# Weaving the transform, the encoder and the last layer of one group into the absolute differences of the next

## The chip, the cores and the metric

One Trainium2 chip, one core. The time is the device time of one execution in microseconds (us). The engines are named as in the profile: PE is TensorE, PEld its weight loads, DVE VectorE, ACT ScalarE, POOL GpSimd; SP is the engine that issues most DMA transfers (524 of 610 in the trace of the kernel before), and its queue (SPq) is called the Sync queue here. The profile's "granted clock" is TensorE's clock as a share of full speed.

## The reference, cut to what matters

An input of 16 batches, 32 channels, 128 x 128, in fp32, goes through four layers, each added to its input after a group normalisation.

```python
x = x + L0(gn(x))    # a row-by-row LSTM
x = x + L1(gn(x))    # absolute differences: out[n,f,i,j] = -sum over c,kh,kw of |q(x) patch - q(w)|
x = x + L2(gn(x))    # 2-D Hartley transform, mixing of 32 x 32 modes, transform back
x = x + L3(gn(x))    # 25 shifted products per channel, 3x3 convolutions with pooling down and up, times x
```

L1 has no product that TensorE could do. For each output channel and tap, VectorE or ScalarE makes relu(q(x) - w) over 128 partitions x 8192 elements (sums of relu and linear terms give the absolute difference), and TensorE only adds the channels up. That is 72 differences for each of 32 halves (16 batches, upper and lower half), 2304 in all. L2 normalises over two channels of one batch and L3 over the same, so what follows L1 can start as soon as a batch is done; the kernel works it off in four groups of four batches.

## The kernel before: the parts that matter

The stages run one after another. In the stage of the differences a batch is first quantised (ScalarE scales, VectorE rounds and clips, the result goes to DRAM with a border), then each half loads its quantised rows four times over, once for each quarter of the partitions.

```python
def jc_rows(t, b, half, n=16 * W):      # 4 blocks of 16 rows x 32 channels -> 128 partitions
    return bass.AP(t.tensor, t.offset + b * CHW + half * 64 * W, [[16 * W, 4], [HW, C], [1, n]])
...
def loaded(b, half):
    q = qp.tile([128, R + 2, P], F16, name="q")
    first = q_d.offset + (b * C * (H + 2) + R * half) * P
    nc.sync.dma_start(q, bass.AP(q_d.tensor, first, [[0, 4], [(H + 2) * P, C], [1, (R + 2) * P]]))
    xr = rp.tile([128, 16 * W], F32, name="xr1")            # the residual, two halves buffered
    nc.sync.dma_start(xr, jc_rows(x1, b, half))
    return q, xr
...
for b in range(B):
    for half in range(2):
        q, xr = following
        following = loaded(b + half, 1 - half)              # (but for the last half)
        if half == 0 and b + 1 < B:
            xq = [unquantised(b + 1, i) for i in range(2)]  # 16 rows each
        ...                                                 # linear terms
        for i in range(72):
            act = i % 4 == 3
            if i == 3 and before:
                finish(*before)                             # residual + sums, statistics, store
            ...                                             # the difference, on ACT or DVE; 16 matmuls
            if i in (10, 30) and half == 0 and b + 1 < B:
                quantise(b + 1, int(i == 30), xq[int(i == 30)])
        before = b, half, acc, xr
```

Of the kernel before, what the change touches and what calls it, by code (L numbers as in the profile page):

```python
# [209 lines left out]
def jc_stats(nc, pool, ps, cst, v, name):  # L210

    rhs = pool.tile([128, NG, 4], F32, name=f"{name}_r")
    nc.vector.tensor_tensor(rhs, bcast(v[:, :], 2, 4), bcast(cst["m4_bc"], 1, NG), ALU.mult)
    p = ps.tile([128, 512], F32, name="acc")
    nc.tensor.matmul(p[:, :16], cst["sel_c"], rhs.rearrange("p g b -> p (g b)"), start=True, stop=True)
    out = pool.tile([128, 16], F32, name=name)
    nc.vector.tensor_copy(out, p[:, :16])
    return out


def jc_rows(t, b, half, n=16 * W):

    return bass.AP(t.tensor, t.offset + b * CHW + half * 64 * W, [[16 * W, 4], [HW, C], [1, n]])


def stage1(nc, tc, keep, cst, sel16, m1, r1, x1, w, q_d, x2):
# [8 lines left out]
    with ExitStack() as ctx:  # L235
        sm = ctx.enter_context(tc.tile_pool(name="s1_sm", bufs=1))
        with tc.tile_pool(name="s1_ps0", bufs=2, space=PSUM) as ps:
            r128 = jc_stats(nc, sm, ps, cst, r1, "r128")
            shift = jc_stats(nc, sm, ps, cst, m1, "shift")
            nc.vector.tensor_scalar(r128, r128, 128.0, None, ALU.mult)  # L240
            nc.vector.scalar_tensor_tensor(shift, shift, -1.0, r128, ALU.mult, ALU.mult)


            qw = sm.tile([128, 72], F32, name="qw")
            nc.sync.dma_start(qw, w)
            top = sm.tile([128, 1], F32, name="top")
            nc.vector.tensor_reduce(top, qw, AX.X, ALU.max, apply_absolute_value=True)
            alltop = sm.tile([128, 1], F32, name="alltop")
            nc.gpsimd.partition_all_reduce(alltop, top, 128, bass_isa.ReduceOp.max)
            scale = sm.tile([128, 1], F32, name="scale")  # L250
            nc.vector.tensor_scalar(scale, alltop, 1.0 / 127.0, 1e-8, ALU.mult, ALU.max)
            nc.vector.tensor_scalar(scale, scale, 2.0**0.5, None, ALU.mult)
            nc.vector.tensor_scalar(scale.bitcast(I32), scale.bitcast(I32), 0x7F800000, None, ALU.bitwise_and)
            nc.vector.reciprocal(scale, scale)
            nc.vector.tensor_scalar(qw, qw, scale, -127.0, ALU.mult, ALU.max)
            nc.vector.tensor_scalar(qw, qw, 127.0, RND, ALU.min, ALU.add)
            nc.vector.tensor_scalar(qw, qw, RND, None, ALU.subtract)
            neg = sm.tile([128, 72], F32, name="neg")
            nc.vector.tensor_scalar(neg, qw, -1.0, None, ALU.mult)


            taps = sm.tile([128, 8], F32, name="taps")
            nc.vector.tensor_reduce(taps, qw.rearrange("p (f t) -> p f t", t=9), AX.X, ALU.add)
            tapb = sm.tile([128, 8, 4], F32, name="tapb")
            nc.vector.tensor_tensor(tapb, bcast(taps[:, :], 2, 4), bcast(cst["m4_bc"], 1, 8), ALU.mult)
            sumw = sm.tile([128, 1], F32, name="sumw")
            p = ps.tile([128, 512], F32, name="acc")
            for j in range(4):
                nc.tensor.matmul(
                    p[32 * j : 32 * j + 32, :1],  # L270
                    tapb.rearrange("p f b -> p (f b)"),
                    cst["ones"][:, :1],
                    start=True,
                    stop=True,
                )
            nc.vector.tensor_scalar(sumw, p[:, :1], 2.0**-7, None, ALU.mult)

        stat = sm.tile([128, B, 8, 6], F32, name="stat2")
        ring = [sm.tile([128, 16, P], F16, name=f"qt{i}") for i in range(2)]
        for t in ring:  # L280
            nc.gpsimd.memset(t, 0.0)
        for row in (0, H + 1):
            nc.sync.dma_start(
                bass.AP(q_d.tensor, q_d.offset + row * P, [[4 * (H + 2) * P, 128], [(H + 2) * P, 4], [1, P]]),
                ring[0].rearrange("p r w -> p (r w)")[:, : 4 * P].rearrange("p (a w) -> p a w", w=P),
            )
        xp = ctx.enter_context(tc.tile_pool(name="s1_x", bufs=2))
        rp = ctx.enter_context(tc.tile_pool(name="s1_r", bufs=2))
        qp = ctx.enter_context(tc.tile_pool(name="s1_q", bufs=2))
        dp = ctx.enter_context(tc.tile_pool(name="s1_d", bufs=2))  # L290
        ps = ctx.enter_context(tc.tile_pool(name="s1_ps", bufs=4, space=PSUM))

        def unquantised(b, half):
            t = xp.tile([128, 16 * W], F32, name="xq")
            nc.sync.dma_start(t, jc_rows(x1, b, half))
            return t

        def quantise(b, half, t):
            nc.scalar.activation(
                t, t, AF.Identity, bias=shift[:, b : b + 1], scale=r128[:, b : b + 1]  # L300
            )
            qt = ring[half]
            nc.vector.tensor_scalar(
                qt[:, :, 1 : W + 1], t.rearrange("p (r w) -> p r w", w=W), RND, RND, ALU.add, ALU.subtract
            )
            flat = qt.rearrange("p r w -> p (r w)")
            nc.vector.tensor_scalar(flat, flat, -127.0, 127.0, ALU.max, ALU.min)
            first = q_d.offset + (b * C * (H + 2) + 64 * half + 1) * P
            nc.sync.dma_start(
                bass.AP(q_d.tensor, first, [[16 * P, 4], [(H + 2) * P, C], [1, 16 * P]]), flat  # L310
            )

        def loaded(b, half):
            q = qp.tile([128, R + 2, P], F16, name="q")
            first = q_d.offset + (b * C * (H + 2) + R * half) * P
            nc.sync.dma_start(q, bass.AP(q_d.tensor, first, [[0, 4], [(H + 2) * P, C], [1, (R + 2) * P]]))
            xr = rp.tile([128, 16 * W], F32, name="xr1")
            nc.sync.dma_start(xr, jc_rows(x1, b, half))
            return q, xr

        def finish(b, half, acc, xr):
            v = [xr[:, 512 * k : 512 * k + 512] for k in range(4)]
            for k in range(4):
                nc.vector.scalar_tensor_tensor(v[k], acc[k], sumw, v[k], ALU.subtract, ALU.add)  # L324
            for k in range(4):
                nc.vector.bn_stats(stat[:, b, 4 * half + k, :], v[k])
            nc.sync.dma_start(jc_rows(x2, b, half), xr)

        for half in range(2):
            quantise(0, half, unquantised(0, half))  # L330
        before = None
        following = loaded(0, 0)
        for b in range(B):
            for half in range(2):
# [19 lines left out]
                for i in range(72):  # L354
# [3 lines left out]
                    if i == 3 and before:  # L358
                        finish(*before)
# [191 lines left out]







# [641 lines left out]
```

## Time and profile before

The median is 8975 us (8941 to 8980). In the profiled execution (8962.7 us) L0 lasts until 1510 us, the differences until 5692, the rest until 8963.

### The profile page before, as it was taken

How to read it: one execution, taken by the hardware profiler on the slowest of the kernel's cores; microseconds unless marked ns; L12 is line 12 of the kernel's file. 1: busy time of each engine (PE TensorE's matmuls, PEld its weight loads, DVE VectorE, ACT ScalarE, POOL GpSimd, SP SyncE). 2: the span in 40 equal slices, each digit the busy share in tenths (PEclk: the TensorE clock that was granted, in tenths of full speed). 3: DMA queues.
4: the chain of work that ended last, by engine and by line, in shares of the span. 5: the costliest groups of instructions: out<-in, count | busy, mean ns of one | idle time of the engine just before them, and what ended most of it. 6: DMA issues, size and time to landing. Idle time of an engine off the chain costs nothing.

```text
span 8962.7 us, 249632 instructions
## 1 busy us (share of the span) xinstructions
PE 6114.4 (68%) x117740; PEld 4037.0 (45%) x117740; DVE 5850.7 (65%) x5842; ACT 5003.2 (56%) x2710; POOL 268.8 (3%) x483
## 2 busy tenths in 40 slices
PE   4999991666666656665665666784656859678955
PEld 3888881222222222222222223584644646455832
DVE  5444432999999999999999999622633232232233
ACT  1444432999999999999999999400000101101122
POOL 0111110000000000000000000000000000000000
PEclk9999995999999999999999999755556859688977
DMA  9799923111111111111111110344721121211077
GB/s 205 53 80 78 82 24 80 42 46 42 42 51 54 44 44 52 39 43 48 54 49 43 41 40 25 121 101 115 244 67 43 37 59 43 59 34 34 27 184 170
DMA packets 1520672, 613.85 MB, mean 68 GB/s; under 512 B 1418269, under 2 KB 1421725, under 8 KB 1491613
## 3 DMA queue, kind: packets, MB, share of 16 engines
q1 hardware_dynamic: 1480636, 518.56, 31.2%
q10 hardware_dynamic: 39008, 79.32, 3.0%
q8 instruction: 922, 15.11, 0.7%
q14 instruction: 106, 0.86, 0.0%
HBM read 433.21 MB, written 164.64 MB: 67 GB/s over the span
## 4 chain that ended last, share of the span: by engine, by line
issue 41%; PE 37%; DVE 14%; ACT 3%; DMA 3%; SPq 1%; another core or an unknown queue 0%; POOL 0%; ACTq 0%; DVEq 0%; POOLq 0%
PE acc L952 10%; DVE d_dve L367 7%; PE pg L174 5%; PE pg L175 4%; PE acc L693 4%; PE acc L612 3%; PE pg L176 3%; PE p L426 2%; ACT d_act L365 2%; PE acc L840 2%; PE pf L526 1%; DVE xr L324 1%; DVE stat L200 1%; PE pa L506 1%; PE p L432 1%
## 5 line engine op out<-in xcount | busy, mean ns | idle before, releaser
L365 ACT ACTIVATE d_act<-q,neg 128x8192 f16<-128x8192 f16 (+1 forms) x576 | 4065.9, 7150 | 54.7 <-PE acc L372 29.9
L367 DVE TENSOR_SCALAR d_dve<-q,qw 128x8192 f16<-128x8192 f16 (+1 forms) x1728 | 3935.0, 2365 | 55.6 <-PE acc L372 32.6
L372 PE MATMUL acc<-d_dve,sel 128*32 128x512 f16 x27648 | 1854.7, 391 | 1317.7 <-DVE d_dve L367 1315.9
L372 PEld LDWEIGHTS <-sel 128*32 128x32 f16 x36864 | 1077.8, 98 | 2786.0 <-issue 2082.7
L952 PE MATMUL acc<-xp,fo_all 32*32 32x512 f32 x25600 | 932.4, 624 | 53.1 <-DVE pooled L853 48.5
L952 PEld LDWEIGHTS acc<-xp,fo_all 32*32 32x32 f32 x25600 | 661.4, 105 | 313.7 <-issue 157.5
L372 PE MATMUL acc<-d_act,sel 128*32 128x512 f16 x9216 | 648.0, 401 | 161.5 <-ACT d_act L365 161.1
L185 ACT ACTIVATE gt<-pg,bias 128x256 f32<-128x256 f32 x1024 | 400.9, 474 | 547.5 <-PE pg L176 547.4
L174 PE MATMUL pg<-h,bd 128*128 128x256 f32 x2048 | 652.7, 401 | 57.8 <-DVE h L194 57.5
L175 PE MATMUL pg<-h,bd 128*128 128x256 f32 x2048 | 623.4, 387 | 0.0
L864 ACT ACTIVATE y<-pooled,fo_b 32x128 f32<-32x128 f32 x256 | 102.4, 400 | 842.8 <-DVE pooled L853 839.4
L980 DVE TENSOR_TENSOR acc<-acc,cut 128x4 f32<-128x4 f32 x256 | 28.7, 166 | 696.4 <-PE acc L952 695.4
L693 PE MATMUL acc<-xp 32*32 32x108 f32 x16384 | 326.8, 376 | 222.1 <-issue 217.1
L176 PE MATMUL pg<-xn,bd 128*128 128x2 f32 (+62 forms) x2048 | 426.1, 289 | 9.6 <-DVE xn L158 9.6
L176 PEld LDWEIGHTS pg<-xn,bd 128*128 128x128 f32 x2048 | 397.2, 194 | 66.8 <-DVE xn L158 10.4
L175 PEld LDWEIGHTS pg<-h,bd 128*128 128x128 f32 x2048 | 398.3, 194 | 56.9
L189 DVE TENSOR_TENSOR c<-c,gt 128x256 f32<-128x256 f32 x256 | 108.6, 424 | 448.7 <-ACT gt L185 448.7
L664 DVE TENSOR_SCALAR xp<-xp,stats 128x2560 f32<-128x2560 f32 (+1 forms) x64 | 101.0, 1580 | 446.9 <-DMA xp<-x_d 446.9
L693 PEld LDWEIGHTS acc<-xp 32*32 32x32 f32 x16384 | 250.4, 134 | 298.8 <-issue 271.1
L174 PEld LDWEIGHTS pg<-h,bd 128*128 128x128 f32 x2048 | 341.9, 195 | 64.7 <-issue 48.4
L347 PE MATMUL acc<-q,sel 32*32 32x512 f16 x4608 | 183.8, 594 | 228.6 <-DVE xr L324 135.0
L669 ACT COPY xp<-xp 128x20 f32<-128x20 f32 x64 | 14.9, 233 | 554.6 <-DVE xp L664 442.8
(234 smaller groups left out, 4693.7 us busy)
## 6 DMA issues: line engine op xcount, KB each, us to landing
xr<-x_d SPq DMA_DIRECT2D x96, 1024.0 KB
q<-q_d SPq DMA_DIRECT2D x32, 2145.0 KB
xp<-x_d SPq DMA_DIRECT2D x48, 1280.0 KB
x_in<-in_x_dram SPq DMA_DIRECT2D x16, 2048.0 KB
res<-in_x_dram SPq DMA_DIRECT2D x32, 1024.0 KB
x_d<-res SPq DMA_DIRECT2D x32, 1024.0 KB
xq<-x_d SPq DMA_DIRECT2D x32, 1024.0 KB
x_d<-xr SPq DMA_DIRECT2D x32, 1024.0 KB
```

The source lines that it names most:

```text
L174: nc.tensor.matmul(pg[:, q], wmat(0, q), h_in[:, :, 1:], start=True, stop=False)
L175: nc.tensor.matmul(pg[:, q], wmat(1, q), h_in[:, :, :H], start=False, stop=False)
L176: nc.tensor.matmul(pg[:, q, :, : t + 1], wmat(2, q), xn[:, 2 * c : 2 * c + 2, j, : t + 1], start=False, stop=True,)
L185: nc.scalar.activation(gt[:, q], pg[:, q], AF.Tanh if q == 3 else AF.Sigmoid, bias=bias[:, q : q + 1])
L347: nc.tensor.matmul(acc[k][32 * j : 32 * j + 32, :], sel16[rows, 8, :], q[rows, row : row + 4, kw : kw + W], start=tap == 0, stop=False,)
L365: nc.scalar.activation(dst, src, AF.Relu, bias=neg[:, i : i + 1])
L367: nc.vector.tensor_scalar(dst, src, qw[:, i : i + 1], 0.0, ALU.subtract, ALU.max)
L372: nc.tensor.matmul(acc[k][32 * j : 32 * j + 32, :], sel16[:, f8, :], d[:, row : row + 4, c : c + W], start=False, stop=i == 71,)
L426: nc.tensor.matmul(p1[:, i, :], xh[:, 16 * half + i, :], cst["cas"], start=True, stop=True)
L612: nc.tensor.matmul(acc[blk][32 * j : 32 * j + 32, : rows * n], self.w[part, par, tap, :], src[part, top : top + rows, left : left + n], st ...
L693: nc.tensor.matmul(gram[blk][32 * j : 32 * j + 32, at : at + 36 * n], xp[rows, l, 2 + 32 * j : 34 + 32 * j], xp[rows, l : l + n, 32 * j : ...
L952: nc.tensor.matmul(acc[blk][32 * j : 32 * j + 32, :], wf["all"][rows, tap, :], xp[rows, 4 * j + kh : 4 * j + kh + 4, kw : kw + W], start=t ...
```

## The change

The work after L1 becomes a generator, and a scheduler lets it go on a little after each difference, by a credit of TensorE time; negative values are holds, so that a dependent piece comes only after a number of differences.

```diff
+class Weave:
+    def advance(self, us, slack):
+        self.credit = min(self.credit + slack, 3.0)
+        self.hold = max(self.hold - us, 0.0)
+        if self.credit < 2.0:
+            return
+        while self.credit > 0 and not self.hold and self.step():
+            pass
+DVE_US, ACT_US, PE_US = 2.26, 7.05, 0.87
...
+                    weave.advance(1.75, 1.75 - PE_US)      # after each difference
...
+        first.run(tc, ctx, weave)                          # the differences
+        weave.drain()                                      # what is left
```

The woven work needs room in SBUF, and so the stage of the differences was rewritten too: pieces of 8 rows in the place of 16, residuals for one half in the place of two, loaded inside the half, three VectorE buffers in the place of four, and the choice of engine by an estimate that counts the woven work.

```diff
-            t = xp.tile([128, 16 * W], F32, name="xq")
+        t = self.xp.tile([128, 8 * W], F32, name="xq")
...
-                    following = loaded(b + half, 1 - half)          # q and residual
-                if half == 0 and b + 1 < B:
-                    xq = [unquantised(b + 1, i) for i in range(2)]
+                    following = self.loaded(b + half, 1 - half)     # q alone
...
+                    if i == 30:
+                        xr = self.residual(b, half)
+                    if half == 0 and b + 1 < B:
+                        if i in (4, 6, 26, 28):
+                            k = (4, 6, 26, 28).index(i)
+                            xq[k] = self.unquantised(b + 1, k)
+                        if i in (20, 24, 40, 44):
+                            k = (20, 24, 40, 44).index(i)
+                            self.quantise(b + 1, k, xq[k])
-                    act = i % 4 == 3
-                    d = dp.tile([128, R, P], F16, name="d_act" if act else "d_dve", bufs=2 if act else 4)
+                    act = weave.act + ACT_US < weave.dve + DVE_US and i < 70
+                    t = dp.tile([128, R, P], F16, name="d_act" if act else "d_dve", bufs=2 if act else 3)
```

The rest of the diff (about 1,700 lines) turns the transform, encoder and last layer into generators of one group with four PSUM banks; it is cut here.

## The prediction

> **What bounds the kernel now.** I read the page first (the slices say which engine is full when), then a table of stretches cut where the stages change, then the groups by shape, then the timeline of TensorE in one group. The four rows of the stretches are the stages: absolute differences (1510 to 5692), transform (to 6470), encoder (to 8594), last layer. Columns: stretch, its length, busy us with instructions for PE, PEld, DVE, ACT, POOL, granted clock, DMA share, GB/s.
>
> ```profile
> PE   4999991666666656665665666784656859678955
> DVE  5444432999999999999999999622633232232233
> ACT  1444432999999999999999999400000101101122
> PEclk9999995999999999999999999755556859688977
> 1510.00:5692.00 4182.00, 2567.51 (x41460) 1182.94 (x41464) 4141.00 (x2049) 4122.26 (x605) 0.00 (x0) 0.94 0.15 44
> 5692.00:6470.00 778.00, 540.90 (x10524) 515.36 (x10516) 286.48 (x366) 32.42 (x45) 7.56 (x50) 0.50 0.54 160
> 6470.00:8594.00 2124.00, 1578.71 (x54284) 1145.82 (x54285) 643.67 (x1878) 242.05 (x644) 30.52 (x170) 0.75 0.18 49
> 8594.00:8963.00 369.00, 220.68 (x5334) 108.11 (x5311) 128.16 (x160) 89.00 (x128) 0.00 (x0) 0.76 0.82 191
> ```
>
> For 4182 us VectorE and ScalarE are full and TensorE is 61% busy; for the next 3271 us it is the reverse, VectorE 32% and ScalarE 11% busy. That is the intent: put the second kind of work under the first. The groups that fill the first stretch, and the two of the second that matter most:
>
> ```profile
> L365 ACT ACTIVATE d_act<-q,neg 128x8192 f16<-128x8192 f16 (+1 forms) x576 | 4065.9, 7150 | 54.7 <-PE acc L372 29.9
> L367 DVE TENSOR_SCALAR d_dve<-q,qw 128x8192 f16<-128x8192 f16 (+1 forms) x1728 | 3935.0, 2365 | 55.6 <-PE acc L372 32.6
> L952 PE MATMUL acc<-xp,fo_all 32*32 32x512 f32 x25600 | 932.4, 624 | 53.1 <-DVE pooled L853 48.5
> L693 PE MATMUL acc<-xp 32*32 32x108 f32 x16384 | 326.8, 376 | 222.1 <-issue 217.1
> ```
>
> There are 1728 + 576 = 2304 differences. By busy time over count one costs VectorE 2.277 us and ScalarE 7.058 us; together they do 1/2.277 + 1/7.058 = 0.581 per us, so 2304 need 3967 us. Other work in this stage (evictions, statistics, quantising) is 226 us on VectorE and 66 on ScalarE. Balanced, T = 3967 + 0.756 D + 0.244 A, where D and A are the other work: 3967 + 171 + 16 = 4154, against 4182 measured. I use this formula for the new stage. Last, TensorE in one group's encoder (start, length, matmuls, idle before):
>
> ```profile
> 7046.42 27.72 PE L952 MATMUL acc<-xp,fo_all 32*32 32x512 f32 x782 [1.12 <-DVE pooled L853]
> 7078.39 27.56 PE L952 MATMUL acc<-xp,fo_all 32*32 32x512 f32 x750 [1.04 <-DVE pooled L853]
> ...
> 7193.98 2.54 PE L693 MATMUL acc<-xp 32*32 32x108 f32 x128 [2.01 <-issue]
> 7197.45 2.54 PE L693 MATMUL acc<-xp 32*32 32x108 f32 x128 [0.93 <-issue]
> ```
>
> The first convolution takes 32 us a chunk of which 28 is matmul; the Gram statistics come in bursts of 128 matmuls, 2.5 us of work each 3.5 to 5 us.
>
> [...] each burst ends in a gap put down to issue. From L693, (327 + 222)/16384 is 33 ns per matmul against 20 ns busy. [...] The differences use 128*32, the woven work mostly 32*32; before has no such alternation, so its trace does not price it. [...] The trace shows 0.94 beside the differences and 0.50 in the transform, though the transform keeps TensorE busy 70% of the time; woven, this work should run at the high clock. [...]
>
> **The change part by part.**
>
> 1. How much is woven. A generator emits transform, encoder and last layer of a group between differences, by credit (0.88 us of TensorE work per difference) and holds. I counted the compiled order: in the stream of differences lie preparing the weights once, group 0 whole, and group 1 without its last layer. After the last difference come group 1's last layer and groups 2 and 3 whole, 20802 of 39634 woven matmuls. Group 0 can start only when its four batches are done, a quarter in, and each group takes some 12 of the 32 halves. So at most about half of the 3271 us can be hidden. The split of differences becomes 1700 to 604.
>
> 2. What it adds to VectorE and ScalarE in the first stage. Per group, from counts in the compiled order times durations by shape in the trace before (or scaled by size from them): mean subtraction 4 x 4.42 = 18; inverse transform 32 x (0.685 + 0.682) = 44; Gram sums 40 halves of about 0.6 = 24; folded weights about 15; pooling 40 x 0.69 + 2 = 29; spreading 40; edge corrections 64 x 0.166 = 11; last layer 64 x 0.45 = 29; small pieces 35: 245 us on VectorE. ScalarE: normalising 16 chunks, moved there from VectorE, about 2.6 each by the 2.09 us of a 2048-wide activation = 42; spreading 50; last layer 25 + 18; the rest 12: 147 us. Preparing: 93 us on VectorE once, in place of folding per group. In the stage: D gains 93 + 2 x 245 - 29 = 554 and A gains 2 x 147 - 43 = 251, so T gains 0.756 x 554 + 0.244 x 251 = 480 us: 4182 becomes 4660.
>
> 3. Stalls, my estimate. Five loads of folded weights (1.47 MB each) stand directly ahead of the VectorE instructions that use them: 35 to 40 us a group. Each of 16 chunk loads stands directly ahead of ScalarE's normalisation: some 8 us each, 130 a group. Some 60 evictions a group follow the matmuls they wait for, half of them in the same burst, about 2 to 3 us: 100. By the same weights, 0.756 x 140 + 0.244 x 130 = 137 a group, but part overlaps and buffers absorb part: 190 for both groups. TensorE: 16 sums back to back take 0.87 us, so with 0.88 of woven work per 1.9 us it is above 90% busy, with 487 returns to the differences' tiling; no separate addition. Stage: 4850, from 1510 to 6360.
>
> 4. The tail, groups 2 and 3. Before, a group cost (778 + 2124 + 369)/4 = 818 us, with groups overlapping each other and eight PSUM banks. Now a group is serial with four banks and two buffers. Transform: four batches at 17 us plus load and statistics 92; round trips of coefficients through DRAM 17; mixing 57 (twice the matmuls of before over all groups, 4096 instructions of 14 ns); then 27 for storing and small-run loads, 35 first inverse, 75 second (16.8 MB at 225 GB/s), 10 statistics: 313 against 195. Encoder: first chunk 12, Gram 133, sums 28, constants 8, folded weights 35, chunk 12, edge 13, eight chunks of 33.5 with exposed eviction 268, rest 100 with exposed eviction: 609 against 531. Last layer: 20 store and load, 95 rounds, 10 end: 125 against 92. Sum about 1030 to 1050. Tail: 2 x 1030 + 125 = 2185.
>
> Sum: 1510 + 4850 + 2185 = 8545; I say 8540, 4.8% under 8975.
>
> **The rivals.** (a) Weaving nearly free: the stalls of step 3 are absorbed, and the tail costs a group what it did before: 1510 + 4660 + 2 x 818 + 92 = 7900. For it: TensorE's 39% idle time and the holds put between dependent pieces. Against: the encoder's own waits (842.8 us of ScalarE waiting for pooling) show chains of short steps that a lone group exposes. (b) In-order blocking: each late woven piece stops VectorE, ScalarE and TensorE in turn, and the woven 24 halves take 170 us rather than 152 (131 before): stage 5200 or more, tail 2250, total 8950, no gain. For it: TensorE and VectorE are both above 90%. Against: three VectorE buffers hold 7 us of slack. [...] (d) DMA: at 44 GB/s in the first stage against 191 to 310 elsewhere there is room.
>
> **Range and chances.** Steps 2 and 1 are firm to 100 us. Step 3 may be 0 to 500, step 4 from 1750 to 2350. Taking most of both: 8150 to 8900. Faster by 2% is under 8796; that needs steps 3 and 4 not to overrun by 250 together: 0.80. Within 2%: 0.15. Slower: 0.05.
>
> **What would show it.** The last difference near 6360 (step 3 wrong if under 6200 or over 6600); then no differences and 2100 to 2250 us with VectorE under a third busy. Halves with only differences near 131 us, woven ones near 152. VectorE idle before the folded weights and ScalarE idle before the normalisation, both released by DMA, in the woven stretch. Granted clock above 0.9 until 6360. Gram bursts in the tail again with issue gaps. I am wrong if the woven halves fill VectorE to 99% (then (a)) or if a tail group takes near 818 us.

## More of the kernel before

The lines that show what is full in each stage are in the prediction. One more is kept here, because it was seen and passed over: the waits of the Sync queue in the stage of the differences (engine and line, released by what, us in all, times, longest).

```profile
SPq L318 <- DMA x_d<-xr: 1223.5, 30, 44.3
```

Once a half, the queue stands for about 41 us at the residual load, until the previous half's result has been stored. One such wait as a stretch of its own (columns as in the prediction; the last three are the granted clock, the DMA share and GB/s):

```profile
2201.00:2243.00 42.00, 29.49 (x498) 13.90 (x475) 42.00 (x25) 40.31 (x7) 0.00 (x0) 0.87 0.25 71
```

VectorE is busy for all 42 us and ScalarE for 40, so the wait costs nothing in the kernel before; the DMA engines are 25% busy throughout. The halves there all take 124 to 137 us (from the start of one half's evictions to the next).

## The result, and the profile after

The changed kernel takes 9418.8 us (9410 to 9420): slower, by a ratio of 1.050 (95% interval 1.0475 to 1.0528). A ratio here is the mean time of one kernel's fast runs over that of the other's of the same rounds, so it isn't quite the ratio of the medians.

The slices of the page of the changed kernel, to be held against those in the prediction (40 slices of 235 us; tenths):

```profile
PE   5999973465445654579977765558987646864496
DVE  5444435697776676699978877678997122222212
ACT  2444425697776676699987777678997001210112
PEclk9999987788787787789988787878998557855597
```

Before, DVE and ACT stand at 9 from one end of the differences to the other. Now they reach 9 in some slices only and fall to 6 and 7 between them, PE with them, so nothing is full there. The stretches, cut at the last difference (columns as in the prediction):

```profile
1483.00:7247.00 5764.00, 3801.75 (x78701) 1817.66 (x78707) 4572.60 (x3424) 4579.03 (x1070) 0.00 (x0) 0.83 0.21 63
7247.00:9418.00 2171.00, 1392.84 (x41749) 1030.97 (x41738) 491.05 (x1198) 327.08 (x504) 0.00 (x0) 0.66 0.33 91
```

The tail is what was predicted (2171 us; predicted 2185). The stretch of the differences is 5764 us, not 4850, although DVE and ACT are busy for only 4573 and 4579 us of it, 79%. The two rows of differences (busy, mean ns, idle before and its releaser) say that their own durations are what they were:

```profile
L463 ACT ACTIVATE d_act<-q,neg 128x8192 f16<-128x8192 f16 (+1 forms) x604 | 4278.0, 7151 | 571.4 <-PE acc L404 534.0
L467 DVE TENSOR_SCALAR d_dve<-q,qw 128x8192 f16<-128x8192 f16 (+1 forms) x1700 | 3906.5, 2357 | 491.4 <-PE acc L404 457.3
```

So each of the two waits for some 1190 us of the stretch (5764 - 4573). The waits (engine, what it was about to do, released by what; us in all, times, longest):

```profile
ACT d_act L463 <- PE acc L404: 534.0, 75, 51.2
ACT xq L361 <- DMA xq<-x_d: 489.6, 25, 55.6
DVE d_dve L467 <- PE acc L404: 457.3, 134, 48.4
DVE qt L364 <- DMA q_d<-qt: 323.6, 15, 56.1
```

The second and fourth are no waits of woven work. They are the differences' own quantising: ScalarE waits for the rows to be loaded, VectorE for the previous rounded piece to be stored, each time for up to 56 us. The first and third are also up to 50 us long, and follow from them: TensorE adds the two engines' differences up in one order, so each engine's stop becomes the other's (at 2548, below, TensorE has stood 51 us for VectorE's next difference). The timeline of one half's start shows how (start, length, engine, line, what; in brackets the idle time before and its releaser):

```profile
2481.45 0.50 SPq L376 DMA_DIRECT2D q<-q_d  x1
2487.28 1.84 SPq L394 DMA_DIRECT2D x_d<-xr  x2
2526.84 5.44 SPq L383 DMA_DIRECT2D xr<-x_d  x2
2532.37 0.54 SPq L368 DMA_DIRECT2D q_d<-qt  x1
2533.00 0.53 SPq L356 DMA_DIRECT2D xq<-x_d  x1
...
2544.80 0.70 DVE L364 TENSOR_SCALAR qt<-xq 128x1024 f16<-128x1024 f32 x1 [49.51 <-DMA q_d<-qt]
...
2549.83 1.24 ACT L361 ACTIVATE xq<-xq,shift,r 128x1024 f32<-128x1024 f32 x1 [54.59 <-DMA xq<-x_d]
```

At 2481 the load of the next half's quantised image goes out, at 2487 the stores of the finished half. The residual load needs those stores' buffers, and the queue stands for 38 us at it. The piece store and the piece load stand behind it in the queue; VectorE and ScalarE stand 50 and 55 us at the pieces, and start no difference until these have come (2545.88 and 2550.97), although TensorE had added up the ones before by 2497. The same moment in the kernel before:

```profile
2194.07 0.51 SPq L316 DMA_DIRECT2D q<-q_d  x1
...
2200.67 0.54 SPq L327 DMA_DIRECT2D x_d<-xr  x1
...
2205.21 2.37 DVE L303 TENSOR_SCALAR qt<-xq 128x2048 f16<-128x2048 f32 x2
...
2243.69 0.51 SPq L318 DMA_DIRECT2D xr<-x_d  x1
```

The queue stands just as long (2201 to 2244), but the two pieces of this batch had been loaded a half earlier and each has a buffer of its own, so the rounding at 2205 waits for nothing.

One more reading: in the 32 us after the stores are issued, VectorE and ScalarE are busy for 8 us and TensorE for 10, and the DMA share is still 0.25.

```profile
2487.00:2519.00 32.00, 10.10 (x224) 5.30 (x216) 7.98 (x12) 8.23 (x3) 0.00 (x0) 0.61 0.25 59
```

A share of 0.25 for the whole wait is what four of the 16 DMA engines, full, would give; that is an estimate from this share alone, and experiment 3 tests it.

### The profile page after: what moved, and what is told of

Read it like the earlier page. It is cut to its first block, busy times and chain, and to the rows that moved or that the text cites. A ratio compares the mean times of both kernels' runs of the same rounds, so it can differ in the third digit from the quotient of the medians.

```text
span 9417.7 us, 268331 instructions
## 1 busy us (share of the span) xinstructions
PE 6396.1 (68%) x126900; PEld 3930.7 (42%) x126900; DVE 5717.8 (61%) x6028; ACT 5425.6 (58%) x2865; POOL 229.3 (2%) x263
## 5 line engine op out<-in xcount | busy, mean ns | idle before, releaser
L463 ACT ACTIVATE d_act<-q,neg 128x8192 f16<-128x8192 f16 (+1 forms) x604 | 4278.0, 7151 | 571.4 <-PE acc L404 534.0
L467 DVE TENSOR_SCALAR d_dve<-q,qw 128x8192 f16<-128x8192 f16 (+1 forms) x1700 | 3906.5, 2357 | 491.4 <-PE acc L404 457.3
L404 PE MATMUL acc<-d_dve,sel 128*32 128x512 f16 x27200 | 1953.5, 419 | 1046.7 <-DVE d_dve L467 1025.2
L404 PE MATMUL acc<-d_act,sel 128*32 128x512 f16 x9664 | 732.7, 426 | 405.5 <-ACT d_act L463 397.6
L1202 PE MATMUL acc<-xp,wf 32*32 32x512 f32 x25600 | 979.8, 617 | 24.1 <-DVE pooled L1128 19.5
L1202 PEld LDWEIGHTS acc<-xp,wf 32*32 32x32 f32 x25600 | 499.4, 104 | 406.3 <-issue 288.5
L361 ACT ACTIVATE xq<-xq,shift,r 128x1024 f32<-128x1024 f32 x64 | 78.1, 1235 | 580.6 <-DMA xq<-x_d 571.5
L583 PE MATMUL acc<-y6l,u_conv 32*32 32x256 f32 x8192 | 335.9, 501 | 90.7 <-issue 43.3
L955 PE MATMUL acc<-xp 32*32 32x108 f32 x16384 | 286.0, 323 | 157.9 <-issue 135.5
L922 ACT ACTIVATE xp<-xp,fr_shift,stats 128x2560 f32<-128x2560 f32 (+1 forms) x64 | 158.8, 2485 | 405.4 <-DMA xp<-x_d 405.4
L1142 ACT ACTIVATE y<-pooled,b 32x128 f32<-32x128 f32 x256 | 102.2, 399 | 408.3 <-DVE pooled L1128 404.2
L955 PEld LDWEIGHTS acc<-xp 32*32 32x32 f32 x16384 | 222.1, 120 | 237.0 <-issue 194.7
L1291 DVE SCALAR_TENSOR_TENSOR xr<-xr,l_mean,s 128x256 f32<-128x256 f32 x256 | 105.4, 482 | 319.5 <-ACT s L1282 269.3
```

The lines of the kernel that those rows point to most:

```text
L404: self.nc.tensor.matmul(acc[k][32 * j : 32 * j + 32, :], self.sel16[:, i // 9, :], d[:, row : row + 4, c : c + W], start=False, stop=i == 71,)
L463: nc.scalar.activation(dst, src, AF.Relu, bias=self.neg[:, i : i + 1])
L467: nc.vector.tensor_scalar(dst, src, self.qw[:, i : i + 1], 0.0, ALU.subtract, ALU.max)
L583: nc.tensor.matmul(acc[blk][32 * j : 32 * j + 32, o : o + rows * n], t[part, 4 * par + tap, :], src[part, top : top + rows, left : left + ...
L922: nc.scalar.activation(v, v, AF.Identity, bias=shift, scale=istd)
L955: nc.tensor.matmul(gram[blk][32 * j : 32 * j + 32, at : at + 36 * n], xp[rows, l, 2 + 32 * j : 34 + 32 * j], xp[rows, l : l + n, 32 * j : ...
```

## The experiments

The theories. A: the 900 us too many are lost by the differences' own rewritten code and its transfers, woven or not. B: they are lost by the weaving: woven pieces come too early, and engines stop at them. All kernels gave correct results. "Nothing woven" means that the generator runs only after the last difference; what the compiled order still moves forward is said under experiment 2. "Stretch" is the time from the first VectorE difference to the end of the last, "tail" the rest, both of the profiled execution.

| run | what | median | ratio to before | stretch | tail |
|---|---|---|---|---|---|
| (before) | | 8975 | 1 | 4180 | 3273 |
| (changed) | | 9419 | 1.050 | 5764 | 2171 |
| e1_resid_pool | residual loads on GpSimd's queue | 9362 | 1.045 | 5715 | 2170 |
| e2_noweave | nothing woven | 10501 | one look | 5248 | 3771 |
| e5_qsplit | image load in four | 8733 | 0.974 | 5099 | 2166 |
| e6_allsplit | all the stage's transfers in four | 8610 | 0.961 | 5011 | 2151 |
| e7_noweave_split | e6, nothing woven | 9570 | one look | 4350 | 3784 |
| e8_noweave_deep | e2, four pieces buffered | 10456 | one look | 4822 | 4162 |
| e9_apart | e6, loads and uses set apart | 8686 | 0.968 | 4981 | 2268 |
| e10_before_split | before, transfers in four | 8900 | 0.992 | 4166 | 3280 |
| e11_lateq | image load moved in the text | 9386 | 1.047 | 5744 | 2158 |
| e12_weave3 | e6, three groups woven | 8418 | 0.939 | 5951 | 1021 |
| e13_weave15 | e6, nearly three groups woven | 8425 | 0.939 | 5695 | 1287 |
| e14_lateq2 | image load held to mid-half | 9068 | 1.010 | 5413 | 2173 |
| e15_lateq_pool | e14, on GpSimd's queue | 9104 | 1.015 | 5432 | 2160 |
| e16_q_pool | image load on GpSimd's queue | 9209 | 1.026 | 5547 | 2167 |
| e17_shortsplit | all but the image load in four | 8889 | 0.990 | 5262 | 2170 |
| e18_lateq_shortsplit | e14 and e17 | 8811 | 0.982 | 5193 | 2165 |

**1. Only the queue's order?**

```diff
-            self.nc.sync.dma_start(xr[i], jc_rows(self.d["x1"], b, half, 8 * i, 8))
+            self.nc.gpsimd.dma_start(xr[i], jc_rows(self.d["x1"], b, half, 8 * i, 8))
```

> The changed kernel, with only the two residual loads of each half issued from the GpSimd queue in place of the Sync queue. In the changed kernel's trace the Sync queue stands about 38 us a half at this load, for the store of the rows that held its buffer; ScalarE's quantising activations then wait some 52 us a half for input. Theory A (that wait on the Sync queue holds up the loads and stores of quantising, and this is most of the 1100 us that the stage lost beyond 480): the differences' stage falls from 5762 to 4900-5300 us, the whole to 8550-8950. Theory B (in-order blocking by woven pieces and TensorE near its limit): stage within 200 us of 5762.

Measured: 9362 us, 57 less, the stretch 5715, within B's range (which only says that A in this form is wrong), and ScalarE still waits 449 us for the pieces. The residual load that stops the queue is part of the sight, not the cause: with it out of the way, the transfers behind it are nearly as late.

**2. Nothing woven.**

```diff
     def advance(self, us, slack):
+        return
```

> The changed kernel with nothing woven: the generator runs only after the last difference. Right result; all four groups in the tail. Theory A (the differences' own new loads, 8-row pieces in two buffers, are what stalls): the stage alone still takes 5500-5900 us, and the total is about 1480 + 5700 + 4 x 1040 = 11300. Theory B (the weave itself stalls): stage near the 4182 of before, total about 9850. Tail of four groups about 1040 each in both, as 2172 us for two groups and a last layer in the changed kernel.

```profile
1481.00:6728.00 5247.00, 2856.90 (x45702) 1355.00 (x45671) 4266.41 (x2498) 4144.29 (x641) 0.00 (x0) 0.83 0.14 44
```

```profile
ACT xq L362 <- DMA xq<-x_d: 897.4, 25, 58.2
DVE qt L365 <- DMA q_d<-qt: 514.5, 11, 52.7
```

With the generator held back the stretch is 5248 us, 1068 more than before, for the same 2304 differences: outside both ranges, but far nearer A's. The stretch isn't quite free of other work. By the trace the compiled order still moves the folding of weights (2037 to 3904 us) and group 0's transform (from 4645 us) forward into it; that is why the tail starts with group 0's encoder and took 3771 us and not 4160. DVE is busy 125 us and ACT 24 us more, about as much of it for the transform as for the folding (e8, where both come later, has 12 and 16 more than before). By the prediction's formula that is worth 0.756 x 113 + 0.244 x 8 = 87 us; 980 us are stalls. They come in whole lumps: 17 of the 31 halves take 169 to 196 us, one 165, the rest 130 to 147. Thirteen of the 17 end before 4640 us, when no group's work has begun. This settles A against B: most of the loss has nothing to do with the weaving.

The same trace holds a control. The compiled order runs the quantising ahead of the program's text, so that the last piece is rounded at 5518 us. The eight halves from 5673 on have no pieces, and take 130 to 134 us, although the collision is there as before: at 5804 the stores go out behind the image load, at 5844 the residual load, and from 5805 to 5840 VectorE and ScalarE are busy for all 35 us with the DMA share at 0.26. So the slow transfers cost time where an engine stands at something behind them, in this trace nearly always a piece (halves of 169 to 196 us), and none where nothing does (130 to 134).

The changed kernel's 5764 is then 4180 + 1068 + 516: the weaving beyond what e2 still overlaps adds 516.

**3. The image load in four.** Its outermost dimension is 4 (a stride of zero over four copies). A share of 0.25 is that of four engines of 16, by the estimate above, and four is also this dimension; whether the two go together is what this run tries. In four transfers of 32 partitions the outermost dimension is 32, and the share should rise.

```diff
-        self.nc.sync.dma_start(q, bass.AP(q_d.tensor, first, [[0, 4], [(H + 2) * P, C], [1, (self.R + 2) * P]]))
+        for j in range(4):
+            self.nc.sync.dma_start(
+                q[32 * j : 32 * j + 32], bass.AP(q_d.tensor, first, [[(H + 2) * P, C], [1, (self.R + 2) * P]])
+            )
```

> The changed kernel, with the 2.1 MB load of the quantised rows of each half as four transfers of 32 partitions in place of one whose outermost dimension is four. The trace shows 0.25 of the DMA engines busy and 58 GB/s for some 37 us after that load is issued, and the store that the residual load waits for queues behind it. Theory A1 (the transfer runs on a quarter of the engines and delays all behind it): the load lands in 10-15 us, the wait at the residual load drops to 15-20 us a half, stage 4900-5300, total 8550-8950. Theory B: stage within 200 us of 5762.

```profile
2430.00:2434.00 4.00, 0.24 (x4) 0.13 (x8) 4.00 (x4) 4.00 (x2) 0.00 (x0) 0.78 0.98 206
```

Measured: 8733 us, the stretch 665 shorter, from this one edit. The stretch and the total are as theory A1 said. The window just after the load's issue has a DMA share of 0.98 (0.29 at the same place in the changed kernel), as nearly all 16 engines would give: that agrees with the estimate; which engines carried the whole load, no trace shows.

**4. All of the stage's transfers in four.** The same edit on the pieces in and out, the residual loads and the stores, which have an outermost dimension of 4 too:

```diff
-    return bass.AP(t.tensor, first, [[16 * W, 4], [HW, C], [1, rows * W]])
+    return [(slice(32 * j, 32 * j + 32), bass.AP(t.tensor, first + 16 * W * j, [[HW, C], [1, rows * W]])) for j in range(4)]
```

> The changed kernel, with every transfer of the differences (unquantised rows, quantised rows out and in, residual, result) split into four of 32 partitions. Theory A1: as for the split of the one load but more, since the store and the small loads also spread: residual wait under 12 us a half, stage 4700-5100, total 8350-8750. Theory B: stage within 200 us of 5762; four times as many issues at about 0.5 us each might even cost a little.

```profile
1431.00:6442.00 5011.00, 3792.79 (x78873) 1810.81 (x78866) 4577.08 (x3439) 4580.12 (x1072) 0.00 (x0) 0.88 0.27 73
```
```profile
ACT d_act L471 <- PE acc L412: 332.5, 77, 15.4
DVE d_dve L475 <- PE acc L412: 288.5, 154, 8.7
...
DVE qt L365 <- ACT xq L362: 37.1, 14, 7.7
ACT xq L362 <- DMA xq<-x_d: 25.8, 10, 6.8
```

Measured: 8610 us, faster than both kernels. DVE and ACT do the same work as in the changed kernel, 753 us sooner. ScalarE's wait for pieces is 26 us in the place of 490; what remains are short waits for TensorE's sums, of 15 us at most.

**5. The same, nothing woven.** (e2's and e6's edits together.)

> Nothing woven, and every transfer of the differences split in four as in the best run so far. Theory A1 (the 1063 us that the differences lose with nothing woven are waits for transfers that run on a quarter of the engines): stage 4180-4350 us, near the 4182 of before; total 9350-9600. Rival (something else in the rewritten differences, such as the choice of engine by estimate or the smaller instructions): stage above 4700, total above 9900.

```profile
1434.00:5785.00 4351.00, 2831.05 (x45882) 1335.53 (x45877) 4266.04 (x2506) 4144.42 (x643) 0.00 (x0) 0.91 0.20 53
```

The stretch is 4350 us: of the 980 us of stalls 898 are gone (5248 - 4350, the halves all at 130 to 151 but one at 162), with the pieces, buffers and order of the changed kernel as they were. By the same subtraction the weaving costs 5011 - 4350 = 661 us.

**6. Depth instead of speed.** The rival inside A: two buffers are too few for four pieces.

```diff
-        self.ring = [sm.tile([128, 8, P], F16, name=f"qt{i}") for i in range(2)]
+        self.ring = [sm.tile([128, 8, P], F16, name=f"qt{i}") for i in range(4)]
...
-        self.xp = ctx.enter_context(tc.tile_pool(name="s1_x", bufs=2))
+        self.xp = ctx.enter_context(tc.tile_pool(name="s1_x", bufs=4))
```

Nothing woven here either; to make room, the stage's buffers are released before the rest starts.

> Nothing woven, transfers as in the changed kernel, but four buffers for the unquantised rows and four for the quantised in place of two and two (as many rows as the kernel before had; they fit because the differences' buffers are released before the rest). Theory A2 (it took both: the slow transfers were there before and were hidden by buffers a half deep; the change halved the buffers): stage 4200-4450, total 9400-9700. Rival A1 alone (depth does not matter): stage 5100-5300, total near 10500.

Measured: the total hardly moves (10456), but the total misleads. The stretch is 4822 us, 426 shorter than e2's and between the two ranges; the folding of weights and group 0's transform (87 us together by the formula) can't start in it for want of released room. They come in the tail, whose 4162 us are 391 more; in its first 400 us TensorE's clock is 0.51. Like for like, depth gives back some 340 of 980 us. The halves show why no more: 12 of them now take 172 to 189 us and the rest 128 to 133. In nine of them the compiled order puts one piece more at the start than there are buffers (all 52 pieces after the first half lie within three differences of an eviction), and the last one waits as long as ever; with more pieces a half there are only fewer such halves. In the other three, which have no pieces left to load, TensorE waits 42 to 53 us for a small load of weights behind the same transfers.

**7. Setting loads and uses apart.** In e6, the normalisation of each chunk moved some matmuls on from its load, and the folded weights fetched two ahead, with more holds.

```diff
-            chunks = [load(0), load(1)]
+            raw = [load(0), load(1)]
+            ready = {0: normalise(raw[0])}
...
-                    for k in range(5):
+                    vs = [fetch(0), fetch(1)]
+                    for k in range(5):
+                        yield -12.0
```

> All transfers split, and two of the prediction's stalls taken away: each chunk's normalisation on ScalarE is emitted most of a chunk after its load in place of directly behind it, and the five loads of folded weights run ahead with pauses between their uses. Theory S (the stalls named in the prediction make up most of VectorE's remaining 434 us of idle time in the stage): stage 4750-4900, total 8330-8500. Rival P (what is left is TensorE nearly full, waits of VectorE and ScalarE for sums): total within 60 us of 8610.

Measured: 8686 us, 76 more than e6: not S, and just outside the 60 of P. The stretch is 30 us shorter, but the added holds leave 21,640 woven matmuls for the tail in the place of 20,802, and the tail is 117 us longer. These loads were no problem in e6 to begin with: in its stretch ScalarE waits 9 us for chunks and VectorE 2 us for folded weights.

**8. The kernel before, split.** The edits of e6 on the old stage.

> The kernel before, with every transfer of the differences split in four. If its deep buffers hid the slow transfers, the stage stays near 4182 and only its start gains (29 us for the first rows, 37 for the first quantised load): total 8850-8950, within 1%. If they were not all hidden: below 8800.

Measured: 8900 us, a ratio of 0.992 (0.9902 to 0.9935). The stretch is 14 us shorter and starts 57 us earlier (1453 for 1510); there the slow transfers delay only the first differences.

**9. Moving the image load in the text.** To get it out of the way of the stores without making it faster:

```diff
-                if (b, half) != (B - 1, 1):
-                    following = self.loaded(b + half, 1 - half)
...
+                    if i == 47 and (b, half) != (B - 1, 1):
+                        following = self.loaded(b + half, 1 - half)
```

> The changed kernel with one thing moved: the load of a half's quantised image (8580 elements a partition, two operations before the stores of the previous half's result in the queue) is issued at the 48th of the 72 differences of a half instead of at its start, so that it has some 28 differences (about 53 us) to land before the next stores, residual loads and quantising pieces are queued. Nothing is split; every transfer keeps its shape and its speed. Theory A (the 1063 us that the rewritten differences lose is time in which short transfers queue behind this one load of about 37 us, and the in-order ScalarE and VectorE stall on them): the stalls go although the load is as slow as before; ScalarE's wait for the loaded pieces falls from 490 us to under 150, the stretch of differences from 5762 to 5000 to 5200, the whole to 8650 to 8850. Rival (the quarter-speed transfers themselves, or the four small quantising pieces in the place of two large, cost the time; splitting helped because it made them quick): the stretch stays above 5600 and the whole above 9250. In between would say that both are in it.

Measured: 9386 us, as the rival said, and yet no evidence for it. In the compiled queue the load stands where it stood, ahead of the stores, and in the trace it goes out at each half's start (2461, then 2467 the stores). Moving the load in the program did not move it in the queue; what it waits for there is its buffer (in the changed kernel 29 times for a difference of VectorE's, 1370 us in all). So a true dependency was needed.

**10. Holding it back.** One element a partition of a difference at or after the 47th is copied into the buffer that the load fills.

```diff
+                        if more and i >= 46:
+                            more = False
+                            nc.vector.tensor_copy(following[:, 0, 0:1], t[:, 0, 0:1])
+                            self.loaded(b + half, 1 - half, following)
```

> The run that moved this load in the program's text alone moved nothing: in the compiled queue and in its trace the load still went out at the start of each half (when the buffer came free), so it told the theories nothing. Here the load is held back by a true dependency: one element a partition of the difference made at or after the 47th of a half is copied into the buffer that the load fills, so the load can't be issued before; by the compiled queue it now stands some 25 differences (47 us) ahead of the next stores and residual loads. All transfers keep their shape and speed, and VectorE has 31 tiny copies more. Theory A (short transfers queue behind the one slow load, and the in-order engines stall): ScalarE's wait for the loaded pieces falls from 490 us to under 150, the stretch of differences from 5762 to 5000 to 5250, the whole to 8650 to 8900. Rival (the transfers' own quarter speed costs the time wherever the load stands): the stretch stays above 5600, the whole above 9250.

Measured: 9068 us, the stretch 351 us shorter: between the two. The wait that first met the eye is gone, from 1087 us to

```profile
SPq L384 <- DMA x_d<-xr: 369.3, 58, 10.8
ACT xq L361 <- DMA xq<-x_d: 281.1, 23, 40.2
```

but ScalarE still waits 281 us for pieces, as the second line shows. Moving the one large load gives back about half of what splitting everything does (351 of 753 us).

**11. Same, on another queue,** since the held load kept the Sync queue standing for 826 us:

```diff
-        self.nc.sync.dma_start(q, bass.AP(
+        self.nc.gpsimd.dma_start(q, bass.AP(
```

> The load of the quantised image held back by the same true dependency to the 47th difference of a half, but issued from GpSimd's queue, so that the one queue of all the other loads no longer stands still until that difference is made (826 us of waiting of that queue in the run before). Theory A (short transfers wait behind the slow load; what was left in the run before came from the queue held by the dependency): the stretch of differences falls from 5413 to 5050 to 5200, near the 5099 of the run with this load split, the whole to 8700 to 8850. Rival (the short transfers' own quarter speed, in a chain of stores, residual loads and pieces at each half's start, is the rest): the stretch stays within 80 us of 5413, the whole at 8990 to 9150.

Measured: 9104 us, stretch 5432, nothing gained, as the rival said. The held queue isn't the rest, unless being on GpSimd's queue cost what that gave; no run separates the two.

**12. The image load at the half's start, on GpSimd's queue.** The same edit on the changed kernel.

> The changed kernel with the load of the quantised image issued from GpSimd's queue, at the start of a half as before, nothing else changed. If the short transfers wait only in the order of the one queue, this frees them: ScalarE's wait for the loaded pieces falls under 150 us, the stretch from 5764 to under 5300, the whole under 8950. If they wait in the DMA engines that this load occupies, whatever queue it came from, the waits stay: the two stores of a half still take some 38 us, the stretch stays above 5600, the whole above 9250. I hold the second for likelier (0.7), since moving the residual loads alone to GpSimd's queue gave back only 49 us.

Measured: 9209 us, stretch 5547, 217 shorter: in between again, and the trace says why. Here is the time from a half's stores to its residual load, in whole us, for the first eleven halves of the stretch's steady part (worked out from the starts in the timeline of the Sync queue):

```
changed kernel   39 41 39 39 39 40 39 42 38 43 39
this run         10 14 38 10 10 10 40 10 10 10 41
```

Three times in four the stores are through in 10 us, every fourth time they take 40 as before. In a half of the first kind, the DMA share while both transfers run is 0.48, as eight engines of sixteen would give (estimated as above), where it was 0.25:

```profile
2431.00:2438.00 7.00, 7.00 (x180) 3.82 (x155) 5.76 (x8) 6.00 (x3) 0.00 (x0) 0.72 0.48 122
```

So the short transfers waited in the DMA engines that they shared with the image load, not in the order of a queue: on another queue the load still kept them for some 40 us in three halves of these eleven, and in the other eight, by my reading of the 0.48, it ran on engines that they didn't use. Why it is every fourth half, no trace shows. My 0.7 for the engines was right, the number that I put to it (above 5600) was not, because it took the load to keep the same engines on either queue.

**13. Only the short transfers in four,** with the image load whole, at the half's start and held back.

> The changed kernel with only the short transfers of the differences split in four (pieces in and out, residual loads, stores of results); the load of the quantised image whole and at the start of a half, as in the changed kernel. If the short transfers lose their time waiting behind that load: their splitting gains little, as splitting them on top of the split load gained 88 us: the stretch 5550 to 5720 against 5764, the whole 9200 to 9370. If their own quarter speed is half of the loss: the stretch 5250 to 5450, the whole under 9100. I hold the first for likelier (0.65).

> The short transfers split in four and the load of the quantised image whole, but held back by the dependency to the 47th difference. No slow transfer is then left at a half's start. If waiting behind the load and the short ones' own speed are all there is: the stretch falls to 5000 to 5130, as with everything split (5011), the whole 8600 to 8740. If it stays above 5300, something else in holding it back costs time (the held queue, the compiled order), and the run that only held it back was no fair measure of the queueing.

Measured: stretches 5262 and 5193. My likelier guess for the first, that their splitting gains little, was wrong: it gains 502 (8889 us). The second (8811 us) missed its range by 63 us, but stayed under the 5300 that would have called for another cause. The table is complete:

| stretch (us) | short transfers whole | in four |
|---|---|---|
| image load whole, at the start | 5764 | 5262 |
| image load whole, held back | 5413 | 5193 |
| image load in four | 5099 | 5011 |

Each cure alone gives back 351 to 665 of 753 us, and they don't add up: the pieces' way is a chain (image load, stores, residual load, pieces) that must be shorter than the slack of the two buffers, and shortening any link does much of it. That reading fits the table, but is argued, not shown. Why holding back leaves 314 us more than splitting, with the stores equally quick, isn't settled; the compiled orders differ there, and holding back stops the queue. The waits show part of it: held back, the load still has others behind it. ScalarE waits 281 us for pieces (135 with the load split), 72 for woven chunks (15) and 71 for the image itself (11). One cure was not run: holding the pieces themselves to the middle of a half, where the program's text has them.

**14. Weaving more.** With the stalls gone, e6 with more credit and shorter holds:

```diff
-        self.hold = max(self.hold - us, 0.0)
+        self.hold = max(self.hold - 2.0 * us, 0.0)        # 1.5 in the second run
...
-DVE_US, ACT_US, PE_US = 2.26, 7.05, 0.87
+DVE_US, ACT_US, PE_US = 2.26, 7.05, 0.45
```

> The kernel with all transfers of the differences split in four (8610 us), with more woven: credit per difference 1.30 us of TensorE work instead of 0.88, and holds counted down twice as fast. By the compiled order, group 2 and the last layer of group 1 then lie under the differences too, and only group 3 (9797 matmuls of 39634) is left behind the last sum, instead of 20802. Theory W (woven groups cost what the runs so far say, 661 us for two, 330 each, against 1010 in the tail): the stretch of differences grows from 5009 to about 5400, the tail falls from 2153 to about 1010, the whole is 7800 to 7950. Rival (the differences have no more room: TensorE, already busy 76% of the stretch, and pieces that come before their input is there, stop the in-order queues): the stretch grows by 900 or more, the whole stays above 8400.

> As the run before it, but holds counted down only 1.5 times as fast: 12299 matmuls are left behind the last sum, that is group 3 and the last layer of group 2 with a little of its first convolution. Theory W: the stretch of differences 5330 to 5400, the tail 1150 to 1250, the whole 7900 to 8050, and some 50 to 150 us slower than the run with holds counted down twice as fast. Rival (shorter holds bring pieces too early, and blocking eats the gain): this one is the faster of the two, because its waits of VectorE and ScalarE for TensorE and for transfers are the smaller.

```profile
1438.00:7388.00 5950.00, 4558.50 (x101030) 2254.88 (x101011) 4823.56 (x4057) 4833.40 (x1357) 0.00 (x0) 0.85 0.29 79
```
```profile
ACT d_act L471 <- PE acc L412: 821.0, 168, 21.9
DVE d_dve L475 <- PE acc L412: 752.7, 332, 18.1
```

Measured: 8418 and 8425 us, the fastest of all (ratio 0.939) and the same as each other. The tail fell as expected (2151 to 1021), but the stretch grew by 940 us for the third group, not by 390. That is what the rival had said for e12 (900 or more, the whole above 8400). W's 330 a group was too low from the start, since e7's stretch, from which its 661 us are counted, already held the folding and group 0's transform. Between e12 and e13 neither was right, since W had e13 slower and the rival had it faster. The waits for TensorE's sums have more than doubled (821 and 753 us against 333 and 289) while TensorE itself is busy 77% of the stretch, as in e6 (76%). So with dense weaving B's mechanism, blocking by woven work, fits: the sums stand in TensorE's order behind woven matmuls that still wait or take long. No run tests this, so it is argued, not shown.

## Why the prediction was wrong, point by point

- **Step 1 (how much is woven): right.** 1700 and 604 differences, and the last difference is followed by groups 2 and 3 and the last layer of group 1.
- **Step 2 (what it adds): right in its numbers, wrong in what it left out; this is the step that failed.** It took "Other work in this stage (evictions, statistics, quantising)" over as 226 and 66 us of busy time, so "4182 becomes 4660" charges the rewritten differences with no waiting at all. Their code was part of the change, and they lose 980 us to stalls in it with the generator held back (e2), of which 898 come back with quicker transfers (e7). (Within the stretch, the lines shown give 4141 - 3935 = 206 and 4122 - 4066 = 56 for the other work; with these the formula gives 4136 and not 4154 for the 4182, which changes nothing else.) The busy times themselves: VectorE has 28 differences fewer, so its other work grew by 4573 - 4141 + 28 x 2.36 = 498 us (554 predicted); ScalarE's by 4579 - 4121 - 28 x 7.15 = 258 (251 predicted; 4121 is its busy time up to 5690 us).
- **Step 3 (stalls of the weaving): right in size, wrong in kind.** Steps 2 and 3 put the weaving at 480 + 190 = 670 us. Measured: 516 in the changed kernel and 661 with quick transfers, and with the 87 us of folding and group 0's transform that lie in the unwoven stretch too, 603 and 748. But the loads that step 3 counts on cost less: 95 us for chunks in the changed kernel and 9 in e6, where it has 130 a group, and 10 and 2 for folded weights, where it has 35 to 40. In e6 the long waits are for TensorE's sums. No run separates what the change between `128*32` and `32*32` matmuls costs; it is inside the 516 to 661 us. (Other than the prediction says, the kernel before has such changes too: its linear terms, L347, are `32*32` matmuls, once a half. The 0.87 us for 16 sums is the distance between two bursts of 16 with no idle time between them in that kernel's trace, 3019.28 and 3020.15.) That the sizes agree is in part luck. In the sum: 980 not foreseen, 66 too much for the weaving, which is 5764 - 4850 = 914.
- **Step 4 (the tail): right,** 2171 against 2185, with small errors of both signs in its parts: by the first loads of each part in the Sync queue, the two groups' transforms take 285 and 291 us (313), the encoders 577 and 586 (609), the last layers 150 and 153 (125). (Its 14 ns an instruction for the mixing is that of L467 in the trace of before, 8192 matmuls and weight loads from 6030.3 to 6145.9 us; its 225 GB/s is an estimate, where that trace has 237 from 6166 to 6470 us.)
- **Rival (d), "at 44 GB/s ... there is room", was the wrong dismissal.** The mean was right and said nothing: with the DMA share at 0.25, the transfers behind the image load still waited some 40 us. The row of the first stretch has the share of 0.15 beside it, and the once-a-half wait of 41 us of the Sync queue was in the trace of the kernel before. A look at one of these waits by itself would have shown 0.25 from end to end, and the four 8-row pieces on two buffers in the diff would have shown who had lost the slack to bear it.
- **Rival (b)** foresaw a stretch of 5200 or more, but by weaving, with TensorE and VectorE above 90% busy; that is not what made it (e2), and TensorE is 66% busy in the stretch. **Rival (a)** fell: woven groups aren't free.
- **What would show it.** The last difference came at 7247, beyond the 6600 that was named as refuting step 3; the fault was one step earlier. Of the 31 halves 19 took some 180 us or more, where 131 and 152 had been expected. The clock was 0.83 in the stretch and not above 0.9; in two undisturbed windows (4250 to 4750 and 6500 to 7000), in which TensorE was busy 93% of the time, it was 0.95, and in the 32 us of a stop shown above 0.61, so the low mean goes with the stops. The Gram bursts kept their gaps: L955 takes (286.0 + 157.9)/16384 = 27 ns a matmul for 17 ns of work, most of the idle time (135.5 of 157.9 us) put down to issue, whose cause no run shows.

## What to carry to other kernels

A change that makes room for itself by smaller pieces and fewer buffers takes away slack that hid slow transfers; before trusting it, look at each wait that costs nothing yet and ask whose buffers keep it so. Look at a transfer's outermost dimension and at the DMA share while it runs, not at the mean over a stage: here an image load that held the share at 0.25 (an estimated 36 us for its 2.1 MB, at the 59 GB/s of the window shown) was a bottleneck at a mean share of 0.14 (e2), and in four transfers it had 0.98. And when a change of two parts fails, run each part alone first: one run with nothing woven told more than any reading of the waits. Look in its trace, too, at whether that part is really gone: here the compiled order had kept a group's transform in.
